# A fused two-layer perceiver kernel: router constants made in an earlier stage, a two-bank start of the causal attention, expert weights loaded in halves, and router steps moved within their slots

## The chip, the cores and the metric

The kernel runs on one core of a Trainium2 chip. The metric is the device time of one execution in microseconds (us); the time shown for a kernel is the median of its runs. Besides the timed runs there is one profiled execution, whose trace gives the start and length of every instruction on each engine: TensorE (PE, with its weight loads as PEld), VectorE (DVE), ScalarE (ACT), GpSimd (POOL) and the DMA queue that SyncE issues (SP). All arithmetic is in 32-bit floating point.

## What is computed

The input x has 64 sequences of 32 rows with 256 features (2048 tokens), and there is a context of 64 x 257 rows with 64 features. Six residual steps follow each other, each on the layer-normed x:

```python
x = x + _L0_xattn_ref(_layernorm(x), ctx_512, ...)   # 16 heads of 16, causal, first 32 context rows matter
x = x + _L0_attn_ref(_layernorm(x), ...)             # 16 heads of 128, one shared key and value
x = x + _L0_ffn_ref(_layernorm(x), ...)              # 16 blocks of 64, the top 4 kept per token
x = x + _L1_xattn_ref(_layernorm(x), ctx_512, ...)   # latent cross attention over 257 context rows, rotary keys
x = x + _L1_attn_ref(_layernorm(x), ...)             # causal, 16 heads of 16, keys and values shared by 4 heads
x = x + _L1_ffn_ref(_layernorm(x), ...)              # 8 experts, each token goes to the best one
```

The last step picks for each token the expert with the largest routing value and applies that expert's gated feed-forward block:

```python
route = jax.nn.sigmoid(x @ router_w)
max_ind = jnp.argmax(route, axis=1)
...
h = jax.nn.silu(x @ gate_w[e]) * (x @ up_w[e])
out = out + jnp.where(mask, h @ down_w[e], 0.0)
```

## The kernel before, in words

The 2048 tokens are 16 tiles x0 to x15 of 128 rows (`xf`, with four more columns for the token's number, its routing value and its norm; `xs` are the 256 features). Four tiles make a group. The stages follow each other; the program names them by letters:

- A (first causal attention), B (second attention, a loop over 16 tiles, from about 172 us), C (blocks of the first feed-forward net, from about 500 us).
- D (cross attention): a loop over 64 blocks b. `score(b)` (L1346) makes scores on PE into two banks, the negated row maximum on DVE (L1364), the exponential on ACT (L1368), its sum's reciprocal (L1376) and the product (L1377) on DVE, which leaves the probabilities `pb`. `turn(b)` transposes them on PE (L1393), `gather(b)` multiplies them with the values (L1416), `project(t)` (L1428) adds the result to x every fourth block. `steps[b]` hangs further work on a block: `ln_group(g, "d")` at block 16(g-1)+1 norms group g (so group 3 at block 33), `half` turns its rows on PE in two parts, two and six blocks later (35 and 39 for group 3); `e_values` at block 53 clears three tiles `vd` on POOL (L1243) and writes their column of ones (L1244); blocks 48 to 62 norm and turn the first rows for stage E.
- E (causal attention), from about 959 us. It has a head (`score(0)`, `values(0)`, `power(0)`, the turn and the queries of group 1) and a loop over slots t = 0 to 14. In slot t the attention of tile t+1 begins and that of tile t-1 ends: `score(t+1)` (64 small matmuls at L306, the mask and maximum on DVE at L257 and L266, the subtraction on POOL at L267), `gather(t-1)` (L1822), `values(t+1)` (L1797), `power(t+1)` (the exponential on ACT, L1789), `heads_on_partitions` of tile t (transposes at L275, copy at L277), `place_values(t+1)` (one copy on DVE at L1813, three on ACT at L1815). Between them `parts` are put in: steps of the next group's features (`transposed_part` L247, `e_features` L1261) and of the router.
- The router works on `ROUTED` sets, (0,1,2,3) and then pairs. `route_stats` takes a tile's statistics on DVE; with the set's last tile `route_scale` makes the norm's factors on POOL (L155, L156, L1594 to L1598). `route_norm` applies them on ACT (L1604), `route_turn` turns the rows on PE (L1618) with a copy on ACT (L1621), `route` makes the choice (L1630, then small DVE operations), `places` ranks the tokens (L1658, L1661), `send` scatters a tile's rows from POOL into the sorted table `srt` in DRAM (L1678). `give_out` makes the expert and row numbers of the next sorted tiles from the counts. `load_expert` (L1529) loads a third of an expert's weights, 512 KB, into `fw`; a DVE memset of one column (L1533) before it sets when SP may issue the load (L1534). Two loads stand at the end of each of slots 0 to 11.
- The expert loop follows (from about 1117 us without router work): 23 sorted tiles, each with gate, up and down matmuls, scattered into the output.

The order of instructions on an engine is the program's where a stage's `manual_schedule` lists that engine: in B it lists PE, DVE, ACT and POOL, in D PE alone, in E PE, DVE and ACT. On the others a scheduler orders them at compile time, after its own estimate of the durations. Tiles of one tag share buffers, so a new tile waits for the last reader of an old one. In stage E each of the accumulator tags "mm", "o", "v" and "PT" is one bank.

The numbers that the router and `give_out` need (`tri`, `one`, `n128`, `n128e`, `ntile`, `token`, `base`) are made between D and E: `numbers` (L1544) counts on POOL (L1546) and converts on DVE (L1548), and 16 POOL copies (L1571) put the token numbers into the tiles' column D. Memory for all these is what stage D has left.

Of the kernel before, what the change touches and what calls it, by code (L numbers as in the profile page):

```python
# [20 lines left out]
NE = 8  # L21
# [24 lines left out]
def perceiver_kernel(ctx: ExitStack, tc: tile.TileContext, a: dict, out: bass.AP):  # L46
# [119 lines left out]
    def stats(mv_slot, src, name):  # L166
        st = sm(f"lnb_{name}", [P, 6])
        nc.vector.bn_stats(st, src)
        nc.vector.bn_aggr(mv_slot, st)
# [34 lines left out]
    def ln_group(g, name, twice=False, act=False, power=False):  # L204

        mv = sm(f"lnm_{name}{g}", [P, 4, 2])
        for i in range(4):
            stats(mv[:, i, :], xs[4 * g + i], f"{name}{g}_{i}")
# [38 lines left out]
    def transposed_part(xn, xT, ps, k, name):  # L247
        tp = ps.tile([P, 512], F32, tag="mm", name=f"tp_{name}_{k}")
# [418 lines left out]


# [57 lines left out]
    with tc.tile_pool(name="wB", bufs=2) as work, tc.tile_pool(  # L726
# [174 lines left out]

        AHEAD = 10
# [69 lines left out]
        for t in range(NT + 1):  # L972
# [40 lines left out]
            place(4)  # L1013
            write_pad(t)
# [208 lines left out]
    with mbw, wd1:  # L1223
# [3 lines left out]
        with tc.tile_pool(name="wD", bufs=2) as work, tc.tile_pool(  # L1227
# [13 lines left out]
            def e_values():  # L1241
                for vd_ in vd:
                    nc.gpsimd.memset(vd_, 0.0)  # L1243
# [17 lines left out]
            def e_features(g, part, o, ps):  # L1261
# [5 lines left out]
                q_ps = ps.tile([P, 512], F32, tag="mm", name=f"qe{g}_{o}_{part}")  # L1267
# [21 lines left out]

            NB = B  # L1290
# [55 lines left out]
            def score(b):  # L1346
# [31 lines left out]
                c0 = 4 * (b % 4)  # L1378
                nc.vector.tensor_tensor(
# [69 lines left out]
            for g in range(1, NG):  # L1449
                b0 = 16 * (g - 1)  # L1450
                steps[b0 + 1] = lambda g=g: lat.update({g: ln_group(g, "d", power=g == 3)})
# [77 lines left out]
    def load_expert(e, n_):  # L1529

        key, k_ = (("f_wg", KC), ("f_wu", KC), ("f_wd", 4))[n_]
        c0 = e * FE + n_ * 1024
        nc.vector.memset(fw[:, c0 : c0 + 1], 0.0)  # L1533
        nc.sync.dma_start(  # L1534
            fw[:, c0 : c0 + 1024].rearrange("p (k i) -> p k i", k=k_),
            a[key][e].rearrange("(k p) i -> p k i", p=P),
        )

    w1 = ctx.enter_context(tc.tile_pool(name="wF1", bufs=1))


    I32 = mybir.dt.int32

    def numbers(name, pattern, mult, n):  # L1544
        i_ = w1.tile([P, n], I32, name=f"{name}_i")
        nc.gpsimd.iota(i_, pattern=pattern, base=0, channel_multiplier=mult)  # L1546
        f_ = w1.tile([P, n], F32, name=name)
        nc.vector.tensor_copy(f_, i_)  # L1548
        return f_

    tri = numbers("tri", [[1, P]], -1, P)
    nc.vector.tensor_scalar(tri, tri, 0.0, None, ALU.is_gt)
    one = w1.tile([P, P], F32, name="one")
    nc.vector.memset(one, 1.0)
    n128 = numbers("n128", [[P, NT]], 0, NT)
# [192 lines left out]
    with tc.tile_pool(name="wE", bufs=2) as work, tc.tile_pool(  # L1748
# [165 lines left out]
        for t in range(NT - 1):  # L1914
# [23 lines left out]
            for fn in parts[3:]:  # L1938
                fn()
# [257 lines left out]
```

## Time and profile before

| What | us |
|---|---|
| median of 3 runs | 1247.11 (1245.01 to 1247.27) |
| profiled execution: time | 1249.61 |
| profiled execution: span from first to last instruction | 1247.6 |
| PE busy in the span | 1178.9 (94%) |
| DVE, ACT, POOL busy | 777.5, 557.9, 367.9 |
| mean granted TensorE clock | 0.953 of full |

The profile's rows are read so. In a timeline a row is a merged run of instructions: start, length, engine, line, operation, output and inputs by the program's names with the buffer numbers left out, shape, count, and in brackets how long the engine was idle before and what released it. "issue" stands where the engine waited for nothing that the profile shows. In a table by stretches the columns are the stretch, its length, the busy time and instruction count of PE, PEld, DVE, ACT and POOL, the granted clock (1.00 is full speed), the busy share of the 16 DMA engines and the rate in GB/s. A wait for several semaphores is put down to the one that came last.

### The profile page before, as it was taken

The numbers are of one execution on the slowest core, as the hardware profiler recorded it, in microseconds if no ns is written. First come the engines' busy times: TensorE is split into PE (matmuls) and PEld (weight loads), VectorE is DVE, ScalarE is ACT, GpSimd is POOL, SyncE is SP. The second block draws the span as 40 slices with busy tenths as digits, with TensorE's granted clock in tenths as the row PEclk, the third lists the DMA queues.
The fourth block names the chain that finished last, engine by engine and source line by source line (L and its number), as shares of the span: only waits on it lengthen the run. The fifth ranks groups of instructions, "written<-read, shape, count | busy, mean of one in ns | idle before, by whom it ended". The sixth has DMA issues, their size and how long they took to land. (4 is left out here: it accounts for less than half of the span.)

```text
span 1247.6 us, 26254 instructions
## 1 busy us (share of the span) xinstructions
PE 1178.9 (94%) x10187; PEld 827.1 (66%) x10187; DVE 777.5 (62%) x1885; ACT 557.9 (45%) x1305; POOL 367.9 (29%) x472
## 2 busy tenths in 40 slices
PE   8999999999999999999989999999999698689997
PEld 5656777677767566777767777767766466555664
DVE  5766257678879966534277777676775465654332
ACT  2337354464554641222365656566654455331111
POOL 2343246675757653000010000010010356432111
PEclk8889999999999989989989999999999888789999
DMA  5121124553454454912141111111100345212110
GB/s 144 48 71 36 29 77 120 148 161 109 133 176 127 135 150 128 269 42 70 34 103 36 50 47 37 48 37 48 38 1 2 103 138 163 66 39 63 38 32 10
DMA packets 94973, 103.11 MB, mean 83 GB/s; under 512 B 37792, under 2 KB 71329, under 8 KB 94626
## 3 DMA queue, kind: packets, MB, share of 16 engines
q1 hardware_dynamic: 92978, 97.19, 27.3%
q0 software_dynamic: 1872, 4.23, 1.0%
q8 instruction: 82, 1.34, 0.4%
q14 instruction: 41, 0.34, 0.1%
HBM read 69.45 MB, written 32.85 MB: 82 GB/s over the span
## 5 line engine op out<-in xcount | busy, mean ns | idle before, releaser
L1368 ACT ACTIVATE pp<-Sd,nm 128x257 f32<-128x257 f32 x256 | 118.0, 474 | 66.5 <-DVE nm L1364 61.3
L775 PE MATMUL qb<-xT_b,b_q 128*128 128x256 f32 x512 | 122.0, 387 | 0.0
L775 PEld LDWEIGHTS qb<-xT_b,b_q 128*128 128x128 f32 x512 | 95.4, 191 | 39.3 <-issue 20.2
L866 PE MATMUL yb<-b_o,oTb 128*128 128x256 f32 x512 | 116.4, 386 | 0.0
L866 PEld LDWEIGHTS yb<-b_o,oTb 128*128 128x128 f32 x512 | 98.4, 194 | 14.3 <-issue 0.7
L1364 DVE TENSOR_REDUCE nm<-Sd 128x2 f32<-128x514 f32 x128 | 83.0, 685 | 23.2 <-PE Sd L1356 23.2
L1377 DVE TENSOR_TENSOR pp<-pp,rd 128x514 f32<-128x514 f32 x128 | 88.8, 694 | 2.1
L1399 ACT COPY pTd<-pt 128x512 f32<-128x512 f32 x112 | 61.4, 598 | 49.6 <-PE pt L1393 49.6
L794 POOL TENSOR_TENSOR q2b<-qTb 128x512 f32<-128x512 f32 x64 | 64.7, 1040 | 27.0 <-ACT qTb L783 15.7
L1416 PE MATMUL od<-pTd,na 128*64 128x256 f32 x480 | 65.2, 392 | 5.6 <-issue 4.3
L1356 PE MATMUL Sd<-ct,qTd 64*128 64x257 f32 x480 | 68.3, 403 | 0.0
L783 ACT COPY qTb<-qb 128x512 f32<-128x512 f32 x64 | 37.4, 585 | 67.8 <-PE qb L775 65.0
L1393 PE MATMUL pt<-cst,pp 128*128 128x128 f32 x512 | 67.3, 275 | 0.0
L1393 PEld LDWEIGHTS pt<-cst,pp 128*128 128x128 f32 x512 | 59.3, 142 | 9.9 <-issue 5.6
L1154 PE MATMUL qd<-xT_d,d_m 128*128 128x256 f32 x256 | 65.3, 399 | 0.2 <-ACT xT_d L242 0.2
L828 DVE RECIPROCAL rqb<-rqb 128x512 f32<-128x512 f32 x16 | 53.5, 3343 | 17.8 <-ACT rqb L823 17.8
L657 PE MATMUL yc<-c,hc 128*128 128x256 f32 x256 | 59.0, 386 | 2.6 <-DVE hc L652 2.6
L1432 PE MATMUL yd<-d_n,co 128*128 128x256 f32 x256 | 59.5, 386 | 0.0
L1154 PEld LDWEIGHTS qd<-xT_d,d_m 128*128 128x128 f32 x256 | 47.3, 194 | 17.2 <-issue 6.0
L842 DVE RECIPROCAL rdb<-denb 128x512 f32<-128x512 f32 x16 | 53.7, 3353 | 5.8 <-PE denb L840 5.6
L657 PEld LDWEIGHTS yc<-c,hc 128*128 128x128 f32 x256 | 49.1, 194 | 12.1 <-DVE hc L652 3.4
L1432 PEld LDWEIGHTS yd<-d_n,co 128*128 128x128 f32 x256 | 47.3, 190 | 11.6 <-issue 5.8
(389 smaller groups left out, 2337.7 us busy)
## 6 DMA issues: line engine op xcount, KB each, us to landing
srt<-pad SPq DMA_DIRECT2D x17, 1040.0 KB
mb<-maskd SPq DMA_DIRECT2D x64, 128.0 KB
ct<-ctd SPq DMA_DIRECT2D x30, 257.0 KB
rct<-in_ctxT_dram SPq DMA_DIRECT2D x32, 128.5 KB
rrt<-in_ctxT_dram SPq DMA_DIRECT2D x64, 64.2 KB
ctd<-rct SPq DMA_DIRECT2D x32, 128.5 KB
nad<-rna SPq DMA_DIRECT2D x16, 256.0 KB
fw<-in_f_wg_dram SPq DMA_DIRECT2D x8, 512.0 KB
```

The lines of the kernel that those rows point to most:

```text
L657: nc.tensor.matmul(y_ps, hs[f][:, i * P : (i + 1) * P], c_2[:, f, :], start=(f == 0), stop=(f == 7),)
L775: nc.tensor.matmul(q_ps[:, hh, :], b_q[:, k, h * P : (h + 1) * P], xT[:, k, c0 : c0 + 256], start=(k == 0), stop=(k == KC - 1),)
L794: nc.gpsimd.tensor_tensor(q2[:, 4 * h4 : 4 * h4 + 4, :], q, q, ALU.mult)
L866: nc.tensor.matmul(y_ps, oT[:, h, :], b_o[:, h, :], start=(h == 0), stop=(h == NH - 1))
L1154: nc.tensor.matmul(q_ps[:, r, :], m[:, k, pr * P : (pr + 1) * P], xT[:, k, c0 : c0 + 256], start=(k == 0), stop=(k == KC - 1),)
L1356: nc.tensor.matmul(s_ps[:, hh, :NKV], qT[hs, b % 8, 4 * u : 4 * u + 4, :], ct[hs, b % 4, :], start=True, stop=True,)
L1364: nc.vector.tensor_reduce(nm, s_ps[:, :, :NKV], AX.X, ALU.max, negate=True)
L1368: nc.scalar.activation(pp[:, hh, :], s_ps[:, hh, :NKV], AF.Exp, bias=nm[:, hh : hh + 1], accum_out=sd[:, hh : hh + 1],)
L1377: nc.vector.tensor_tensor(pp, pp, bc(rd, 2, NKV), ALU.mult)
L1393: nc.tensor.transpose(pt[:, hh * 256 + u * P : hh * 256 + u * P + P], probs[b][:, u, hh, c * P : (c + 1) * P], ident,)
L1416: nc.tensor.matmul(o_ps[64 * hh : 64 * hh + 64, 0, :], na[:, j, c, :], pT[:, c, hh * 256 : (hh + 1) * 256], start=(c == 0), stop=(c == 1),)
L1432: nc.tensor.matmul(y_ps, co[:, pr, :], n[:, pr, :], start=(pr == 0), stop=False)
```

## The change

It has six parts.

1. Constants. `count_up` makes the five counted tiles on POOL at the start of stage B, `all_numbers` converts them on DVE at the end of slot 2 of B into tiles that live to the end; the second count for `n128e` falls away. The 16 copies of token numbers go one by one to the ends of B's slots 3 to 16 (two in slots 3 and 16).
2. Head of E. The first turn and the queries of group 1 take two banks ("mm" and "o") in place of one; the turn stands ahead of `power(0)`, and `score(1)` stands between the turn and the queries instead of at the start of slot 0.
3. Stage D. `stats` of group 3 gets a `sign`: DVE first copies a value of the latest block's probabilities into the statistics' tile, so that the norm can't be scheduled before that block. `e_values` gets such a copy on POOL ahead of each memset. At block 33 the latest block is 34, at block 53 it is 54.
4. Weights. `load_piece` loads half of what `load_expert` did (256 KB), with its own memset; four pieces stand spread over a slot instead of two loads at its end.
5. Router in E. `route_norm` moves to the begin of its slot, right behind the scores (in slot 8 it stays behind the second part). `route_turn` does both halves at once, behind the slot's other parts: for a pair of tiles in one bank with one copy, for the first set of four in two banks.
6. Scatters. The sends move to slots 9 to 13, one behind the scores and one behind `gather`; tiles 10 and 11 are sent after the loop.

```diff
-    def stats(mv_slot, src, name):
+    def stats(mv_slot, src, name, sign=None):
         st = sm(f"lnb_{name}", [P, 6])
+        if sign is not None:
+            nc.vector.tensor_copy(st[:, 0:1], sign)
         nc.vector.bn_stats(st, src)
...
+    def count_up(pool):
+        counted = {}
+        for name, (pattern, mult, n) in COUNTS.items():
+            i_ = counted[name] = pool.tile([P, n], I32, name=f"{name}_i", bufs=1)
+            nc.gpsimd.iota(i_, pattern=pattern, base=0, channel_multiplier=mult)
+        return counted
+
+    def all_numbers(counted):
+        made = {}
+        for name, i_ in counted.items():
+            made[name] = const.tile(list(i_.shape), F32, name=name)
+            nc.vector.tensor_copy(made[name], i_)
+        tri = made["tri"]
+        nc.vector.tensor_scalar(tri, tri, 0.0, None, ALU.is_gt)
+        one = const.tile([P, P], F32, name="one")
+        nc.vector.memset(one, 1.0)
+        n128e = const.tile([P, NT], F32, name="n128e")
+        nc.vector.tensor_scalar_add(n128e, made["n128"], float(P - 1))
+        return tri, one, made["n128"], n128e, made["ntile"], made["token"], made["base"]
...
+            if t == 2:
+                tri, one, n128, n128e, ntile, token, base = all_numbers(counted)
+            if t > 2:
+                for t_ in {3: (0, 1), NT: (NT - 2, NT - 1)}.get(t, (t - 2,)):
+                    nc.gpsimd.tensor_copy(xf[t_][:, D : D + 1], token[:, t_ : t_ + 1])
             write_pad(t)
...
             def e_values():
                 for vd_ in vd:
+                    nc.gpsimd.tensor_copy(vd_[:, 0, 0, 0, 0:1], lately["p"])
                     nc.gpsimd.memset(vd_, 0.0)
...
+                lately["p"] = pb[:, 1, 1, 0:1]
...
-                steps[b0 + 1] = lambda g=g: lat.update({g: ln_group(g, "d", power=g == 3)})
+                steps[b0 + 1] = lambda g=g: lat.update(
+                    {g: ln_group(g, "d", power=g == 3, sign=lately["p"] if g == 3 else None)}
+                )
...
+    pieces = iter([(e, n_, h) for e in range(NE) for n_ in range(3) for h in range(2)])
+
+    def load_piece():
+
+        e, n_, h = next(pieces, (None,) * 3)
+        if e is None:
+            return
+        key, k_ = (("f_wg", 1), ("f_wu", 1), ("f_wd", 2))[n_]
+        c0 = e * FE + n_ * 1024 + h * 512
         nc.vector.memset(fw[:, c0 : c0 + 1], 0.0)
         nc.sync.dma_start(
-            fw[:, c0 : c0 + 1024].rearrange("p (k i) -> p k i", k=k_),
-            a[key][e].rearrange("(k p) i -> p k i", p=P),
+            fw[:, c0 : c0 + 512].rearrange("p (k i) -> p k i", k=k_),
+            a[key][e].rearrange("(k p) i -> p k i", p=P)[:, h * k_ : (h + 1) * k_, :],
         )
...
+    def route_turn(ts, work, ps, tags):
+
         n_ = len(ts)
+        xn = rows[ts]
+        xT = work.tile([P, KC, n_ * P], F32, tag="xTf", name=f"xTf{ts[0]}", bufs=1)
+        rows[ts] = xn, xT
+        ks = 4 // n_
+        for k0 in range(0, KC, ks):
+            tp = ps.tile([P, ks, n_ * P], F32, tag=tags[k0], name=f"tpf{ts[0]}_{k0}")
...
+            nc.scalar.copy(xT[:, k0 : k0 + ks, :], tp)
...
-        sends = {
-            8: (0, 1), 9: (2, 3), 10: (4, 5), 11: (6, 7), 12: (8, 9), 14: (10, 11)
-        }
+        sends = {9: (0, 1), 10: (2, 3), 11: (4, 5), 12: (6, 7), 13: (8, 9)}
...
+        e_group_start(1)
+        for k in range(KC):
+            transposed_part(lat[1], feats[1][2], ps1, k, "e1", ("mm", "o")[k])
+        score(1)
         power(0)
-        for fn in group(1, 0) + group(1, 1):
-            fn()
         place_values(0, v_ps.pop(0))
+        for o in range(KC):
+            e_features(1, 1, o, ps1, ("mm", "o")[o])
         for t in range(NT - 1):
...
-            score(t + 1)
+            if t > 0:
+                score(t + 1)
+            load_piece()
+            if t in steps_n and t % 4 > 0:
+                route_norm(steps_n[t])
+            for t_ in sends.get(t, ())[:1]:
+                send(t_)
             for fn in parts[:1]:
                 fn()
             if t > 0:
                 gather(t - 1)
-            if n_own < 2 and t in steps_n:
-                route_norm(steps_n[t])
+            load_piece()
+            for t_ in sends.get(t, ())[1:]:
+                send(t_)
             for fn in parts[1:2]:
                 fn()
-            if n_own > 1 and t in steps_n:
+            if t in steps_n and t % 4 == 0:
+
                 route_norm(steps_n[t])
...
             for fn in parts[3:]:
                 fn()
+            if t in steps_n:
+                route_turn(steps_n[t], work, ps2, ("mm", "o"))
             place_values(t + 1, v_ps.pop(t + 1))
-            for n_ in range(2 * t, 2 * t + 2):
-                if n_ < 3 * NE:
-                    load_expert(n_ // 3, n_ % 3)
+            load_piece()
...
                 route_stats(t - 1)
-            for t_ in sends.get(t, ()):
-                send(t_)
+            load_piece()
...
         gather(NT - 2)
+        for t_ in ROUTED[-3]:
+            send(t_)
         rows_turn(0)
```

## The prediction

> **What bounds the kernel now.** I read the page's 40 slices first, then busy time by stage, then the waits of the last attention stage, then the timeline at each long wait. All times are us from the span's start.
>
> The slices (engine, busy tenths; PEclk is the granted TensorE clock):
>
> ```profile
> PE   8999999999999999999989999999999698689997
> PEclk8889999999999989989989999999999888789999
> ```
>
> TensorE is busy nearly everywhere, except in slices 31 to 36, where its clock drops as well. Busy time by stage (stretch, length, busy time and count of each engine, clock, DMA share, GB/s):
>
> ```profile
> 627.00:959.00 332.00, 323.11 (x2194) 232.65 (x2194) 240.10 (x594) 203.74 (x666) 12.63 (x19) 0.99 0.17 41
> 959.00:981.40 22.40, 16.31 (x236) 9.24 (x234) 4.80 (x19) 4.19 (x8) 3.75 (x23) 0.77 0.01 2
> 981.40:1087.80 106.40, 85.19 (x2502) 62.77 (x2503) 65.85 (x233) 52.85 (x113) 56.46 (x99) 0.84 0.42 138
> 1117.00:1247.60 130.60, 123.15 (x476) 77.08 (x474) 52.74 (x135) 22.13 (x43) 24.86 (x27) 0.99 0.12 37
> ```
>
> Cross attention (627 to 959) and the expert loop (from 1117) are TensorE at full clock: nothing is won there by moving other engines' work. The causal attention loses time twice, to waits and to the clock: 22.4 us of head (score(0) to values(1)), 106.4 us of loop over slots t. The head (start, length, instruction, idle before and its releaser):
>
> ```profile
> 965.32 1.95 POOL L1571 COPY x<-token 128x1 f32<-128x1 f32 x16 [0.31 <-DVE token L1548]
> 968.31 0.63 ACT L1789 ACTIVATE s_e<-s_e 128x512 f32<-128x512 f32 x1 [9.90 <-POOL s_e L267]
> 969.46 0.72 PEld L250 LDWEIGHTS tp_e<-cst,xn_e 128*128 128x128 f32 x4 [3.48 <-ACT xT_e L251]
> 971.25 3.78 PE L1269 MATMUL qe<-xT_e,e_q 128*128 128x512 f32 x4 [0.68 <-ACT xT_e L251]
> 981.40 0.94 PEld L1797 LDWEIGHTS ve<-e_v,xT_e 128*32 128x32 f32 x64 [1.32 <-ACT vde L1815]
> ```
>
> One bank and one queue make a chain: token copies, POOL's subtract, the exponential, and only then ACT's copy that frees the bank for the second turn. The waiting TensorE goes to half clock, so four query matmuls take 3.78 instead of 1.98 us (the same group at 1006.68). In the loop:
>
> ```profile
> 994.75 0.28 PE L306 MATMUL S_e<-kde,qTe 32*32 32x64 f32 x7 [2.35 <-issue]
> 999.52 0.37 PE L1797 MATMUL ve<-e_v,xT_e 128*32 128x64 f32 x2 [2.54 <-issue]
> 1050.71 0.57 PE L1618 MATMUL tpf<-cst,xn_f 128*128 128x128 f32 x2 [1.67 <-ACT xTf L1621]
> 1074.40 1.09 ACT L1604 ACTIVATE xn_f<-x,lnq_f 128x256 f32<-128x256 f32 x2 [4.08 <-POOL lnq_f L1596]
> 1075.06 0.97 PE L1618 MATMUL tpf<-cst,xn_f 128*128 128x128 f32 x2 [4.63 <-ACT xn_f L1604]
> ```
>
> The first two waits are for nothing the program does; the third is one bank turned twice; the last waits for POOL, whose norm chain (1069.78 to 1074.4) has two scatters of 1.06 and 1.04 us inside it. Stage starts matter too; cross attention begins so:
>
> ```profile
> 624.90 1.95 POOL L1243 MEMSET vde<- 128x1088 f32 x2 [118.98 <-PE yc L657]
> 629.58 0.16 DVE L183 SCALAR_TENSOR_TENSOR lnh_d<-lnm_d,lnr_d 128x4 f32<-128x4 f32 x1 [2.40 <-POOL lnr_d L156]
> 631.46 0.50 PEld L1356 LDWEIGHTS Sd<-ct_d,qTd 64*128 64x128 f32 x4 [3.54 <-ACT pp L1368]
> ```
>
> VectorE stands at the group 3 norm, which stands behind POOL's memsets of vd; the first row maximum (L1364, 629.66) stands behind it.
>
> **Start of cross attention.** The memsets and the norm both leave this place: each now reads block probabilities of late blocks. The maximum can follow its scores at about 627.85, so the chain gains 1.8 (629.66 - 627.85); what is late next is ACT's table load, until 628.43, which allows that. The clock was half from 631.0 to 637.9; two groups there took 2.14 and 3.78 instead of 1.14 and 1.99, 2.8 in all. Whether it stays up is open (0 to -2.8); I take half: -1.4.
>
> **The norm put at block 34.** It brings to VectorE 4 copies (0.1), 4 statistics (0.43 + 0.18, overlapping, 0.5 a pair) = 2.4, then POOL's 0.23 + 1.04, then four rows at 0.47. Probabilities of block 34 are ready at 802.6 and the turn of group 3 (half(0)) needs the rows at 811.99. 802.7 + 2.4 + 1.0 (x add and statistics already there) + 1.4 + 0.2 + 1.9 = 809.6; the row maxima of the next block, at 806.91 now, stand behind it: 2.7 late, of which 1.9 (pp done 810.63, used 812.49) is slack. +1.0, between 0 (the scheduler interleaves) and +3. The vd memsets at block 54 are 3 x (1.03 + 0.3) on a POOL that is 4% busy; only VectorE can feel them: +0.3 (0 to 1). The added waits: VectorE's copy waits for VectorE itself, so for nothing; POOL's copy waits for block 54, and behind it stand only bias adds (917) and the memsets, which nobody needs before 966.
>
> **Constants moved to the second stage.** Five iotas (0.15 to 0.24 each), 8 VectorE operations of 0.17 to 0.25 (1.5) at slot 2, and 16 POOL copies of 0.12. There (212 to 232) TensorE is busy 20.00 of 20 us and POOL idles 6.1 of 20; behind the 1.5 on VectorE stand gather(2)'s copies at 230.19, whose user (L866) starts at 235.0. Covered: 0; uncovered it is +1.5 once.
>
> **Head.** Without casts the mask add starts when the scores end, 964.8 for 965.35. With two banks and the copies ahead of the exponential on ACT, in order: turns 965.6 to 966.9, xT copies to 967.6, score(1) to 967.8 (its bank is free from 965.5), queries 2 x 1.98 at full clock to 971.8, values(1) at 971.8 for 981.40. Placing value 0 on ACT (968.3 to 970.9, after VectorE's copy) is over by then. -9.6; as slot 1's oe must wait for ACT a little, -9.5 (-7.5 if the clock drops, -10).
>
> **Loop.** Weight pieces: bytes per slot are the same, 48 issues of about 0.4 on SP and 48 memsets of 0.06 on VectorE instead of 24; SP has nothing else until the rows at 1083. The two issue waits are instruction blocks: 16 of 16 KB are loaded in 979.4 to 1062.9 (the DMA answer), one per 256 instructions, while 1 MB of weights is queued. The Trainium skill, "Runtime: NRT & Kernel Launch", section "Instruction fetch mechanics", calls a block crossing "mostly hidden": by it pieces are worth 0; by the rows 4.9 us can go. The third block, with less ahead of it, started 1.1 us after its turn, the two before 2.2 and 2.3 after. I take 2 x 1.2 = -2.5, as a dense 256 instructions take about 2.3 us and no fetch is that short.
> Turns: route_turn for two tiles is one bank and one 512 copy, at the slot's end; waits of 1.15 (1034.32) and 1.67 (1050.71) go. -2.3, the longer copy (0.60 for 2 x 0.37) hidden behind the next scores.
> Norms ahead and scatters later: the 4.63 goes, as POOL runs the chain (1.9) unsplit and ACT has the whole slot. POOL per slot is then 1.06 + 0.74 + 2 x 1.2 + 1 = 5.2, under a slot's 5.5 to 8. ACT, in order, may wait at slots 11 and 13 for that chain; behind it stands only the exponential, needed a slot later.
> The clock comes on top:
>
> ```profile
> 1047.50:1050.90 3.40, 1.57 (x12) 1.25 (x12) 2.24 (x11) 2.46 (x6) 2.61 (x4) 1.00 0.84 274
> 1050.90:1061.10 10.20, 9.65 (x214) 8.03 (x214) 4.36 (x14) 4.58 (x11) 5.78 (x13) 0.50 0.43 135
> ```
>
> The Trainium skill, "TensorE: Matmul & The Clock Gate", section "HAM oscillation", gives as rule no idle gap over about 3.4 us. Here a gap of 1.67 in a window busy 1.57 of 3.40 is followed by 10.2 us at half clock. By the rule slot 10's gap is worth 1.67; by the rows another 9.65/2 at most. I take the rows, but 3.0 of it, since others pace slot 11 too. Slot 13 took 11.8 (1067.39 to 1079.19), 10.3 of it at clock 0.50, with work like slot 12's 6.5: -5.5.
> Loop: -2.5 - 2.3 - 3.0 - 5.5 = -13.3 (-6 to -20). Late next: VectorE's give(10) chain (16 operations, 1079.3 to 1082.6), then instruction blocks. After 1087.8: 0 (-2 to 1); VectorE's give(12) still holds the bank there.
>
> **Sum.** -1.8 - 1.4 + 1.0 + 0.3 - 9.5 - 13.3 = -24.7. The profiled execution took 1249.6 (span 1247.6), 2.5 over the median of 1247.1: 1249.6 - 24.7 - 2.5 = 1222.
>
> **Rivals.**
> Gaps only (0.20): the clock windows fall badly and fetches stay. -1.8 + 1.3 - 7.5 - 1.15 - 1.67 - 4.6 = -15: 1232. For it: the clock's 3.4 us windows have no fixed phase.
> Clock up throughout (0.18): -4.1 - 10 - 19 - 2 = -35: 1212. Against it: matmuls of 8 columns (L1630) precede a cold window at 1023.6 though TensorE was busy.
> Little done (0.05): POOL is not ordered by hand here; scatters land in the chain again, and the head's gain goes to later waits: 1246.
> Slower (0.11): instruction starvation. The loop's 5005 TensorE instructions are 19.6 blocks. Pieces keep weight traffic always ahead of a fetch, where now some fetches meet an empty queue. The loaded period was 4.77 (994.75 to 999.52); from 6.0 on, 118 us, the gains of head and start are eaten; at 6.3 it is 123.5: 1253. Against it: slots 11 to 14 carry almost no weights.
> Likeliest, as summed: 0.46, own range 1214 to 1230.
>
> **Numbers.** Range 1208 to 1240: it takes in the first three but for edges (0.03), and leaves out 0.05 + 0.11. About 0.2% is what a measurement of this kernel tells from no change. Faster 0.84, within 0.2% 0.05, slower 0.11.
>
> **What would show it.** Right: values(1) follows the queries without a half-clock group, about 9 us earlier; L1618's waits under 1 us; issue waits after the fourth slot under 1.5 each; L1364 starts under 1 us after the first scores. Wrong: issue waits in several slots; POOL's scatters between L155 and L1596; half(0) waiting for xn_d by over 3 us.

## The result and the profile after

The changed kernel takes 1231.11 us (median of 6 runs, 1225.71 to 1232.89), the kernel before 1246.86 in the same comparison (1239.95 to 1249.26): ratio 0.9874, 95% interval 0.9842 to 0.9906. So it is faster by 1.3%, inside the range of the prediction (1208 to 1240), 9 us above the predicted 1222 and 1 above the narrower range (1214 to 1230) of its likeliest case. The profiled execution took 1230.48, its span is 1228.4.

The 40 slices of the changed kernel's page:

```profile
PE   8999999999999989999999999989999988799997
PEclk8889999999999998988999999999999988889999
```

The weak stretch at the end of the row is shorter than before and its clock is 8 where 7 stood. By stage, in the columns of the table shown for before (cross attention, head up to the start of values(1), loop over slots, expert loop):

```profile
629.00:961.00 332.00, 321.19 (x2194) 230.42 (x2194) 240.05 (x604) 203.92 (x666) 16.01 (x24) 1.00 0.17 41
961.00:973.20 12.20, 11.96 (x238) 8.06 (x234) 4.33 (x12) 3.36 (x7) 2.10 (x2) 1.00 0.05 9
973.20:1068.80 95.60, 81.23 (x2506) 61.68 (x2506) 66.18 (x256) 53.41 (x111) 55.49 (x99) 0.89 0.51 153
1096.70:1228.40 131.70, 123.22 (x476) 77.03 (x474) 52.76 (x134) 22.14 (x43) 24.66 (x27) 0.99 0.12 37
```

Head and loop of the causal attention now take 12.2 and 95.6 us where they took 22.4 and 106.4. The head's instructions, in the timeline:

```profile
967.79 1.09 PE L252 MATMUL tp_e<-cst,xn_e 128*128 128x128 f32 x8
969.60 3.70 PE L1309 MATMUL qe<-xT_e,e_q 128*128 128x512 f32 x8
973.23 0.94 PEld L1825 LDWEIGHTS ve<-e_v,xT_e 128*32 128x32 f32 x64 [0.76 <-ACT vde L1843]
```

Eight transposes run together, the eight query matmuls take 3.70 at full clock (four took 3.78 before), and values(1) follows after 0.76. At the start of cross attention the first row maxima (VectorE) now follow their scores (TensorE) by 0.85, where they came 2.48 after them:

```profile
629.10 1.14 PE L1397 MATMUL Sd<-ct_d,qTd 64*128 64x257 f32 x8 [0.68 <-ACT qTd L1200]
629.95 1.29 DVE L1405 TENSOR_REDUCE nm<-Sd 128x2 f32<-128x514 f32 x2 [1.17 <-PE Sd L1397]
```

For the experiments I cut each profile at the same instructions: **C** from the last normed tile of stage B to the clearing of `plast`; **D start** from there to the `plast` product of block 2; **D middle** from there to that of block 62 (the expectations below call this "from the fourth block to the last"); **E head** to the first copy of turned heads; **loop** to the sixteenth such copy, with the time at half clock inside it; **rest** to the end. The `plast` product is a small one on VectorE that ends each block of D. A cold window is a stretch in which the granted TensorE clock is 0.50.

| profile | C | D start | D middle | E head | loop (half clock) | rest | span | median |
|---|---|---|---|---|---|---|---|---|
| before | 131.9 | 17.1 | 305.6 | 34.4 | 106.9 (36.1) | 157.1 | 1247.6 | 1246.9 |
| changed | 133.8 | 13.1 | 309.9 | 23.6 | 95.9 (20.5) | 157.5 | 1228.4 | 1231.1 |
| E1 norm free | 137.1 | 15.3 | 305.6 | 23.6 | 96.6 (18.6) | 157.8 | 1230.8 | 1228.8 |
| E2 two loads | 137.1 | 13.1 | 309.9 | 23.6 | 99.8 (27.3) | 156.5 | 1230.0 | 1231.4 |
| E3 old router | 137.1 | 13.1 | 309.9 | 23.6 | 112.9 (47.8) | 154.4 | 1245.1 | 1239.5 |
| E4 head alone | 131.9 | 17.1 | 305.6 | 23.6 | 108.6 (34.1) | 154.3 | 1233.6 | 1239.9 |
| E5 late weights | 137.1 | 13.1 | 309.9 | 23.6 | 94.4 (21.9) | 157.9 | 1230.6 | 1230.3 |
| E6 norm spread | 137.1 | 13.1 | 307.4 | 23.6 | 96.6 (21.7) | 158.0 | 1228.4 | 1226.5 |
| E7 old scatters | 133.8 | 13.1 | 309.9 | 23.6 | 97.9 (25.4) | 157.8 | 1226.0 | 1232.3 |
| E9 all spread | 137.1 | 13.1 | 307.9 | 23.6 | 97.8 (27.3) | 154.8 | 1226.9 | 1229.8 |
| E10 rows on GpSimd | 137.1 | 13.1 | 307.4 | 23.6 | 95.2 (20.5) | 156.5 | 1227.4 | 1227.3 |
| E11 no vd sign | 133.2 | 14.5 | 309.0 | 23.6 | 95.4 (17.5) | 156.4 | 1218.7 | 1229.1 |
| E12 vd sign alone | 131.9 | 15.0 | 305.6 | 32.0 | 106.6 (24.4) | 156.1 | 1241.9 | 1243.5 |
| E13 slack blocks | 134.6 | 14.5 | 305.4 | 23.6 | 95.1 (20.5) | 157.0 | 1220.1 | 1222.7 |

A median carries about 0.3% (4 us), while D middle and the new E head repeat to 0.1 in every profile with the same instructions there, if no cold window falls into them. Small steps are therefore read from stage lengths, and medians only say whether the sum agrees. Stages A and B (486.5 to 494.8) are not in the table: they differ between profiles by their cold windows.

### The profile page after: what moved, and what is told of

Same layout as the page of the kernel before. It is cut to its first block, busy times and chain, and to the rows that moved or that the text cites. A ratio compares the mean times of both kernels' runs of the same rounds, so it can differ in the third digit from the quotient of the medians.

```text
span 1228.4 us, 26334 instructions
## 1 busy us (share of the span) xinstructions
PE 1169.0 (95%) x10187; PEld 822.6 (67%) x10187; DVE 778.2 (63%) x1912; ACT 557.7 (45%) x1299; POOL 369.4 (30%) x474
## 3 DMA queue, kind: packets, MB, share of 16 engines
q8 instruction: 82, 1.34, 0.5%
## 5 line engine op out<-in xcount | busy, mean ns | idle before, releaser
L808 PEld LDWEIGHTS qb<-xT_b,b_q 128*128 128x128 f32 x512 | 95.4, 191 | 39.3 <-issue 20.2
L1474 PEld LDWEIGHTS yd<-d_n,co 128*128 128x128 f32 x256 | 47.3, 190 | 11.6 <-issue 5.8
```

Source lines behind the costliest of these rows:

```text
L808: nc.tensor.matmul(q_ps[:, hh, :], b_q[:, k, h * P : (h + 1) * P], xT[:, k, c0 : c0 + 256], start=(k == 0), stop=(k == KC - 1),)
L1474: nc.tensor.matmul(y_ps, co[:, pr, :], n[:, pr, :], start=(pr == 0), stop=False)
```

## The experiments

**E1, the norm of group 3 without its sign.** The vd signs stay.

```diff
-                    {g: ln_group(g, "d", power=g == 3, sign=lately["p"] if g == 3 else None)}
+                    {g: ln_group(g, "d", power=g == 3)}
```

> The changed kernel without the sign in group 3's norm (the copy of a probability that holds the norm until block 34); the three signs of the vd memsets stay. Theory A: the norm at block 34 costs the row maxima of two blocks 4.8 us (the stretch of D from the 800.1 to the 825.4 us of the changed kernel takes 25.3 against 20.5 before), so without the sign that stretch takes 20.5 to 21.5 again. At the start of D the norm stands on VectorE again, but POOL, freed of the memsets, answers in 1.3 us: at most +1.3 there. Net -3.5: 1227.5. Theory B: the 4.8 comes from the statistics of stage E's groups, which the scheduler has put into the same blocks, and goes nowhere without the sign: the stretch stays at 24 to 25 and the start gets later by 1: 1232.

1228.84 (ratio to before 0.9848, 0.9810 to 0.9886). D middle is 305.6, exactly that of before, so theory A holds: without the sign the 4.3 are gone. D start is 15.3, 2.2 more than in the changed kernel, and a cold window of 3.4 us falls into it. The changed kernel's own rows show how the 4.3 arise. A norm here is a tile's statistics (`lnb`, `lnm`) on VectorE, a factor (`lnr`) on GpSimd, a second factor (`lnh`) and the rows (`xn`) on VectorE. In the kernel before, these were the row maxima of block 35 and of block 36 (VectorE), and the scores and product behind the first of them (TensorE). VectorE had stood 1.47 for a factor of stage E right ahead of the first, but TensorE lost nothing by it:

```profile
806.91 1.28 DVE L1364 TENSOR_REDUCE nm<-Sd 128x2 f32<-128x514 f32 x2
810.75 1.29 DVE L1364 TENSOR_REDUCE nm<-Sd 128x2 f32<-128x514 f32 x2
```

```profile
809.91 1.14 PE L1356 MATMUL Sd<-ct,qTd 64*128 64x257 f32 x8
810.98 1.08 PE L1416 MATMUL od<-pTd,na 128*64 128x256 f32 x8
```

In the changed kernel, whose clock of events is here 2.5 us ahead, the same queue holds:

```profile
800.21 0.27 DVE L169 COPY lnb_d<-pp 128x1 f32<-128x1 f32 x3
...
804.35 0.16 DVE L185 SCALAR_TENSOR_TENSOR lnh_d<-lnm_d,lnr_d 128x4 f32<-128x4 f32 x1 [1.17 <-POOL lnr_d L156]
...
804.77 1.66 DVE L196 SCALAR_TENSOR_TENSOR xn_d<-x,lnr_d,lnh_d 128x256 f32<-128x256 f32 x4
806.34 1.29 DVE L1405 TENSOR_REDUCE nm<-Sd 128x2 f32<-128x514 f32 x2
...
811.30 0.16 DVE L185 SCALAR_TENSOR_TENSOR lnh_e<-lnm_e,lnr_e 128x4 f32<-128x4 f32 x1 [0.92 <-POOL lnr_e L156]
...
816.96 0.16 DVE L185 SCALAR_TENSOR_TENSOR lnh_e<-lnm_e,lnr_e 128x4 f32<-128x4 f32 x1 [1.24 <-POOL lnr_e L156]
```

The maxima at 806.34 stand behind all four statistics, VectorE's wait of 1.17 for GpSimd's factors, and four rows, so they come 1.9 late (806.34 + 2.5 - 806.91). ScalarE's exponentials wait for them, and TensorE's next scores wait for the exponentials to empty their two banks. That happens twice, and a wait put down to "issue" follows:

```profile
808.20 0.70 PE L1397 MATMUL Sd<-ct,qTd 64*128 64x257 f32 x4 [0.71 <-ACT pp L1409]
...
810.08 1.14 PE L1458 MATMUL od<-pTd,na 128*64 128x256 f32 x8 [0.26 <-ACT pTd L1441]
...
813.70 0.70 PE L1397 MATMUL Sd<-ct,qTd 64*128 64x257 f32 x4 [1.03 <-ACT pp L1409]
...
821.86 1.08 PE L1458 MATMUL od<-pTd,na 128*64 128x256 f32 x8 [1.00 <-issue]
```

In the kernel before, TensorE has no gap over 0.3 us from 800 to 824. Behind the held norm it reaches the product at 810.08 late by 1.6 (810.08 + 2.5 - 810.98). The other 2.7 of the 4.3 come at the second and third place, and there the queue stands behind the two `lnh_e` rows: the scheduler has also moved stage E's statistics and factors behind the held norm, where before it had spread the statistics singly, one about every 20 us. VectorE waits 0.92 and 1.24 for GpSimd's factors of stage E, and the next maxima stand behind each. The wait of 1.00 at 821.86 ends right after VectorE's last reading of that bank (L1370, at 821.48 and 0.28 long), so I put it down to the same queue. The sign brings the norm and stage E's factors there together, and E1 takes both away, so this split is read from the rows and not tested by itself.

**E2, the old weight loads.** Two loads of 512 KB at the end of a slot in place of four pieces.

```diff
-            load_piece()
...
+            for n_ in range(2 * t, 2 * t + 2):
+                if n_ < 3 * NE:
+                    load_expert(n_ // 3, n_ % 3)
```

> The changed kernel with the old weight loads: two of 512 KB at the end of a slot, one memset each. Theory A (the prediction): pieces shorten two waits for instruction blocks by 1.2 each; with the old loads the loop of slots takes 98.4 in place of 95.9 between the first and the last copy of turned heads, and 1233.6 in all. Theory B: pieces are worth nothing, as the changed kernel still has such waits of 3.10 and 2.12 in it: 95.9 within 1, and 1231 in all, with one or two issue waits of 2 to 3 at other places.

1231.38 (0.9877, 0.9836 to 0.9918), no difference in the median. In slots 1 to 7 the waits for instructions on TensorE are 1.80 and 1.23 here, 0.96, 3.10 and 2.12 in the changed kernel: pieces don't shorten them, so theory B for the waits. The loop of this one profile is 3.9 longer, with 6.8 more at half clock. Loops with the changed instructions span 95.9 to 97.8 (changed, E1, E6, E9), so 99.8 lies outside, and theory A named 98.4; whether it would come again one profile can't say, and 2.5 us of a median are under its noise.

**E3, the router's norm, turn and scatters at their old places.**

```diff
-            if t in steps_n and t % 4 > 0:
-                route_norm(steps_n[t])
...
+            if n_own < 2 and t in steps_n:
+                route_norm(steps_n[t])
...
-            if t in steps_n:
-                route_turn(steps_n[t], work, ps2, ("mm", "o"))
...
+                fns += [lambda k=k: route_turn(steps_n[t], k, work, ps2, "mm") for k in range(KC)]
```

> The changed kernel with the router's norm, turn and scatters at their old places in the slots (pieces, head, constants and stage D as changed). Theory A (the prediction): turns 2.3, slot 11's clock 3.0 and slot 13 5.5 come back, so the loop takes 106.7 in place of 95.9 and the whole 1242; the turn waits for POOL's norm by over 3 us at slot 13. Theory B: the loop is faster because it starts warm and without a debt behind the head, and the router's places are worth only the two turn waits: the loop takes 98 to 100, the whole 1234 to 1235.

1239.46 (0.9944, 0.9917 to 0.9971): 8.4 slower than the changed kernel. The loop took 112.9, 17 longer, 47.8 of it at half clock. Slot 13's wait is back (TensorE):

```profile
1074.97 0.97 PE L1642 MATMUL tpf<-cst,xn_f 128*128 128x128 f32 x2 [5.19 <-ACT xn_f L1628]
```

Theory A. The places of the router's steps are the main part of the loop's gain, about 8 by the medians; the 17 of one profile holds clock windows that need not fall so again.

**E4, the head alone on the kernel before,** with the constants in stage B.

```diff
-        power(0)
-        for fn in group(1, 0) + group(1, 1):
-            fn()
+        e_group_start(1)
+        for k in range(KC):
+            transposed_part(lat[1], feats[1][2], ps1, k, "e1", ("mm", "o")[k])
+        score(1)
+        power(0)
```

> The kernel before with only the constants moved to stage B and the head of E in two banks. Theory A: the head is worth 9.5 by itself and what follows keeps its length (the loop's 106.9, D's as before): 1237.4. Theory B: later waits of the loop (the POOL chain of slot 13, instruction blocks) take up a good part of it: the loop gets longer than 110, the whole 1242 to 1245.

1239.86 (0.9957, 0.9925 to 0.9990), 5 to 7 better than before; E head 23.6 in place of 34.4, the loop 108.6 in place of 106.9. The head is worth 10.8 in its own stage, and nothing else has to change for that. Whether 1.7 is given back in the loop one profile can't say. By order of size theory A.

**E5, no weights in slots 0 to 4.**

```diff
+        if t < 5:
+            return
         e, n_, h = next(pieces, (None,) * 3)
```

(and two pieces at each place from slot 5 on)

> The changed kernel with no weight piece in slots 0 to 4 of stage E; from slot 5 on two pieces stand where one stood, so that all 48 are asked for by slot 10. Theory A (the prediction): the waits for instruction blocks in slots 1 to 4 (1.28 and 2.55 in one profile, 0.96 and 3.10 in another of the changed kind) come from weights queued ahead of the block, and with no weights there they fall under 0.5 each. Theory B: a block that is fetched while 32-row matmuls rush by can't come in time by itself, weights or not: both waits stay, 1 to 3 us each, and the time stays within 3 of the changed kernel's 1231.

1230.27 (0.9821, 0.9770 to 0.9872). The waits fall from 0.96, 3.10 and 2.12 to one of 0.62, one of 1.34 (TensorE) and none near slot 6:

```profile
990.88 0.27 PE L1827 MATMUL ve<-e_v,xT_e 128*32 128x64 f32 x2 [1.34 <-issue]
```

For slots 1 to 4 this repeats: the waits over 0.6 us sum to 0.93 to 2.40 in the four profiles without weights there (E5, E10, E11, E13) and to 3.03 to 4.89 in the ten others. Past slot 4 it doesn't: with the same weights, now two pieces at each place, E10, E11 and E13 wait 2.70, 2.13 and 2.39 in slots 5 to 8. The loop is the shortest of all, 94.4, against 95.1 to 95.4 in those three. The DMA view of 975 to 1003 in 40 slices of 0.7 us shows instruction blocks and nothing else until the weights start:

```profile
GB/s 0 0 0 0 23 0 0 0 0 23 0 0 0 0 23 0 0 0 0 23 0 0 0 0 23 0 0 0 0 23 0 0 0 23 0 0 85 246 392 217
q8 instruction: 7, 0.11, 1.4%
```

One 16 KB block every five slices: the trace has them at 985.25, 988.62, 992.01, 995.44 and 998.79, 3.4 us apart. In the changed kernel they lie 3.8 to 5.0 apart over the same slots (978.64, 982.48, 986.63, 991.58, 996.21), with 198 GB/s on the queues. So both theories hold in part: weights delay the blocks, as A said, but a wait of 0.6 to 1.6 us stays without them. Whether 3.4 us is the time of a fetch or the pace at which TensorE uses blocks up is not shown. What such a wait costs beyond itself is seen in the changed kernel. First its two rows on TensorE, then the clock windows around the first of them:

```profile
989.82 0.37 PE L1825 MATMUL ve<-e_v,xT_e 128*32 128x64 f32 x2 [3.10 <-issue]
...
1018.87 0.30 PE L308 MATMUL S_e<-kde,qTe 32*32 32x64 f32 x5 [2.12 <-issue]
```

```profile
985.80:989.20 3.40, 0.92 (x66) 0.76 (x55) 1.63 (x6) 0.63 (x1) 1.75 (x3) 0.99 0.69 180
989.20:996.00 6.80, 6.18 (x136) 4.61 (x139) 3.82 (x13) 2.84 (x7) 3.37 (x4) 0.50 0.53 159
```

TensorE was busy 0.92 of 3.40 us, and the next 6.8 us ran at half clock. In E5, whose wait was 1.34, no window in slots 1 to 5 was cold (clock 1.00 over 979 to 1000), and none was in E10, E11 and E13, whose longest wait there was 1.55.

**E6, group 3's norm spread**: one tile's statistics at each of blocks 24 to 27, the scale at 28, one row at each of 29 to 32.

```diff
+            for i in range(4):
+                steps[24 + i] = lambda i=i: stats(mv3[:, i, :], xs[12 + i], f"d3_{i}", lately["p"])
+                steps[29 + i] = lambda i=i: out3(i)
+            steps[28] = scale3
```

> The changed kernel with group 3's norm of stage D spread over blocks: one tile's statistics at each of blocks 24 to 27, the scale at 28, a row at each of 29 to 32, all held by a sign of their block; the scheduler still puts stage E's eight statistics behind the last row in one bundle. Theory A: the 4.3 that the norm at block 34 costs is the length of the norm's own chain ahead of half(0); spread, the way from the fourth block to the last takes 305.6 to 306.5 in place of 309.9, the start keeps its 13.1 (17.2 before), and the whole is 1227. Theory B: about half of it is stage E's statistics, which stay in a bundle: 308, and 1229.

1226.48 (0.9824, 0.9794 to 0.9854). D middle 307.4, so 2.5 of the 4.3 are back and 1.8 stay, all of which arises at blocks 29 to 31. By size it is theory B; its reason is tried next.

**E9, stage E's statistics spread as well.**

```diff
+            for i in range(8):
+                steps[(36, 37, 38, 40, 41, 42, 43, 44)[i]] = lambda i=i: stats(
+                    mve[i // 4][:, i % 4, :], xs[i], f"e{i // 4}_{i % 4}", lately["p"]
+                )
```

> As the kernel with group 3's norm spread, and stage E's statistics of groups 0 and 1 also held by signs, one tile at a time at blocks 36 to 44. Theory A (the norm's own chain is the cost): the same 305.6 to 306.5 from the fourth block to the last, no more gained: 1227. Theory B (half of it is the bundle of stage E's statistics): 306 here against 308 with group 3's norm spread alone: 1227 against 1229. Either way the best kernel so far, if the rest stays.

1229.81 (0.9852, 0.9823 to 0.9880), D middle 307.9; up to block 32 the delay is 2.0, as in E6 (1.9). The bundle of stage E's statistics is not what stays: both theories miss.

**E10, the rows on GpSimd**, on top of E6, with E5's weights.

```diff
-                lat[3].append(ln_out(xs[12 + i], *lat["s3"], i, "d3"))
+                nc.gpsimd.tensor_scalar(
+                    y, xs[12 + i], rs3[:, i : i + 1], sh3[:, i : i + 1], ALU.mult, ALU.add
+                )
```

> The kernel with group 3's norm spread, its four rows (blocks 29 to 32) now on GpSimd in place of VectorE, and the weights as in the kernel that loads none in slots 0 to 4. Theory A: the 1.9 that the spread norm still costs between blocks 28 and 32 is VectorE's time for four rows of 0.47 in a chain where VectorE paces the blocks; on GpSimd, 4% busy there, they are free: from the fourth block to the last 305.6 to 306; with the loop's 94.4 the whole is 1222 to 1224. Theory B: it is the wait of the factors (lnh_d behind GpSimd's power) that holds VectorE, and stays: 307.4, and 1225. Theory C: GpSimd's rows take over 1.2 each and half(0) waits for them: over 308.

1227.31 (0.9831, 0.9799 to 0.9862), D middle 307.4: the rows weren't it either; theory B. Two rows of this kernel, VectorE's and then TensorE's:

```profile
779.41 0.16 DVE L185 SCALAR_TENSOR_TENSOR lnh_d<-lnm_d,lnr_d 128x4 f32<-128x4 f32 x1 [0.67 <-POOL lnr_d L156]
...
781.53 0.27 DVE L1370 TENSOR_TENSOR lT<-od,maskj 128x128 f32<-128x128 f32 x1
```

```profile
781.90 1.08 PE L1458 MATMUL od<-pTd,na 128*64 128x256 f32 x8 [1.65 <-issue]
```

VectorE stands for GpSimd between the two halves of block 29's product. Right behind that product it has a copy and the masking at 781.53 to do, and TensorE's wait of 1.65, put down to "issue", ends 0.1 after that masking has read the bank. There is little slack at that place: in the kernel before, VectorE idled 0.51 us up to the product of block 29 and 0.58 up to that of block 30, but 2.54 for block 27, 1.56 for 28, 2.56 for 31 and 3.59 for 35 (summed from its timeline between `plast` products).

**E13, each statistic in a block with slack,** and the factor `lnh` on GpSimd too, on top of E10; stage E's eight statistics are spread over six such blocks.

```diff
+                nc.gpsimd.tensor_tensor(sh, mv[:, :, 0], rs, ALU.mult)
+                nc.gpsimd.tensor_scalar(sh, sh, -1.0, None, ALU.mult)
...
+                steps[(21, 22, 25, 26)[i]] = lambda i=i: stats(
+                    mv3[:, i, :], xs[12 + i], f"d3_{i}", lately["p"]
+                )
```

> As the kernel with GpSimd's rows and late weights, but each statistic of group 3's norm in a block where VectorE idled over 1.5 us in the trace of before (blocks 23, 24, 27, 28), stage E's eight statistics likewise (blocks 31, 32, 35, 39, 40, 43), and the factor lnh of these norms on GpSimd, so that VectorE waits for GpSimd nowhere in these blocks. Theory A: what is left of the cost of the norm (1.8, all of it between blocks 28 and 31) is the place: VectorE has 0.5 us of slack in blocks 29 and 30 and its queue stood 0.67 for lnh_d there. With this the way from the fourth block to the last takes 305.6 to 306.0, as with no norm there at all, the start keeps 13.1, and the whole is 1223 to 1225, the fastest of all. Theory B: the statistics cost VectorE's path at any place: 307 to 308, and no faster than 1226.

1222.70 (0.9812, 0.9778 to 0.9846), D middle 305.4, as with no norm there. Theory A by its size; place and `lnh` changed together, so what each is worth stays open. VectorE in block 27 of this kernel:

```profile
757.64 0.43 DVE L170 BATCH_NORM_STATS2 lnb_d<-x 128x6 f32<-128x256 f32 x1
758.10 0.18 DVE L171 BATCH_NORM_AGGREGATE lnm_d<-lnb_d 128x2 f32<-128x6 f32 x1
759.13 0.42 DVE L1484 TENSOR_TENSOR x<-x,yd 128x256 f32<-128x256 f32 x1 [0.85 <-PE yd L1477]
760.65 1.29 DVE L1405 TENSOR_REDUCE nm<-Sd 128x2 f32<-128x514 f32 x2 [1.09 <-PE Sd L1397]
```

The maxima still wait for their scores, 1.09: the statistics lie in time that was idle. This is the fastest version by its median, 0.6% under the changed kernel (0.9812 / 0.9874), though the two intervals touch.

**E7, only the scatters at their old places.**

```diff
-        sends = {9: (0, 1), 10: (2, 3), 11: (4, 5), 12: (6, 7), 13: (8, 9)}
+        sends = {
+            8: (0, 1), 9: (2, 3), 10: (4, 5), 11: (6, 7), 12: (8, 9), 14: (10, 11)
+        }
```

> The changed kernel with the scatters at their old places (two at the end of slots 8 to 12 and 14), the norm and the turn of the router as changed. Theory A (the prediction): scatters inside the norm's chain on POOL make the 4.6 to 5.2 wait at slot 13; with them back there, the turn of slot 13 waits over 2, and the loop takes 100 to 103 in place of 95.9 to 96.6: 1236. Theory B: the norm at the slot's begin and the turn at its end are what removes the wait, since the chain then has the whole slot: no turn waits over 1, the loop within 1.5 of 96.3: 1231.

1232.32 (0.9889, 0.9848 to 0.9931), loop 97.9. One turn waits, that of slot 13:

```profile
1057.09 1.39 PE L1644 MATMUL tpf<-cst,xn_f 128*128 128x128 f32 x4 [2.06 <-ACT xn_f L1628]
```

Ahead of it GpSimd's chain is split again, with two scatters in it:

```profile
1052.53 1.06 POOL L1706 DMA_INDIRECT srt<-x,slots  x1 [0.50 <-POOL lnr_f L155]
1053.61 0.74 POOL L156 TENSOR_TENSOR lnr_f<-lnr_f,mhalf 128x2 f32<-128x2 f32 x1
1054.54 1.05 POOL L1706 DMA_INDIRECT srt<-x,slots  x1 [0.18 <-issue]
```

Between the two: the wait is there as A has it, but with 2.06 in place of 5.19 (E3), and the loop is 0.1 to 3.5 longer than those with all the changed places (94.4 to 97.8). The scatters' place is worth about 2 us at slot 13, not to be told from nothing by the median, and the norm's and turn's place the rest: a turn at the slot's end leaves the split chain time to finish.

**E11, without the vd signs,** on top of E10, and **E12, the vd signs alone** on the kernel before (the same line, put in).

```diff
-                    nc.gpsimd.tensor_copy(vd_[:, 0, 0, 0, 0:1], lately["p"])
                     nc.gpsimd.memset(vd_, 0.0)
```

> As the kernel before this one in the list, without the three signs ahead of the vd memsets, so the memsets stand at the start of stage D again, 4 us of GpSimd. Theory A: with no norm there, nothing of VectorE stands behind GpSimd, the start keeps its 13.1 and the whole its time (within 1); the vd signs are worth nothing once the norm is away. Theory B: [...]the order makes the first row maxima later: 14 to 17. As to stage C, whose length follows its cold clock windows alone (131.9 in the two profiles without vd signs, 133.8 to 137.1 in the eight with them): if the signs set it, 131.9 here; if it is chance, any of the three.

1229.06 (0.9852, 0.9823 to 0.9880). The first maxima start 1.16 after VectorE's queue is free for them, with the scores, as in the changed kernel (1.17); D start is 14.5 because a cold window of 3.4 us falls into it. So the vd signs are worth nothing once the norm is away. D middle is 309.0, 1.6 over E10 and all of it at the product of block 31, behind another cold window of 3.4 us.

> The kernel before with only the three signs of the vd memsets. Theory A: at the start of D the norm waits for GpSimd's factors 1.3 in place of 2.4 and more, and the start takes 15.3 as in the changed kernel without the norm's sign (17.1 before); everything else as before: -1.8, 1245. Theory B: nothing, since the clock is cold there in both: 17.1 and 1247. Stage C: 131.9 if its cold windows are chance, 133.8 to 137.1 if the signs set them.

1243.47 (0.9981, 0.9955 to 1.0007), not to be told from before by its median. D start 15.0: the factors come after 1.54 in place of 2.40, as A has it. E head is 32.0 for 34.4 because fewer cold windows fell there. Stage C is 131.9 with the signs, so they alone don't set its length.

## Why the prediction was right, step by step

The direction was right and for the main reasons given. By the profiled executions the sum was -24.7 and the measure is -19.1; the other 3 us of the 9 are the step from profile to median: I took 2.5 off, but the changed kernel's profile lies 0.6 under its own median. Of the signs that the prediction named, the queries ran at full clock, the router's turns in the loop waited 0.47 at most and the first maxima came 0.85 after their scores; but instruction waits stood in several slots, one of 2.12 after the fourth.

- **Start of cross attention**, -3.2 predicted, -4.0 measured (17.1 to 13.1). The waits gave 1.7, near the 1.8 of the prediction: counted from the clearing of `plast`, the first maxima start after 3.4 before, after 2.5 in E1 and in E12, and after 1.7 in the changed kernel, so 0.9 is GpSimd's memsets and 0.8 the norm. The other 2.3 are the clock, of which I took half of 2.8: 6.8 us at half clock fall there before, 3.4 in E1 and E12, none in the changed kernel. Some of that is luck: E11 and E13 have neither wait, but 3.4 us at half clock there, and take 14.5.
- **The norm at block 34**, +1.0 (0 to +3) predicted, +4.3 measured: this step failed, in two places. The queue itself went as worked out, even a little better: the maxima came 1.9 late and not 2.7. First, "of which 1.9 is slack" was wrong. I took it at the transposes of `pp`, the last user of the exponentials; the first users are the next block's scores, which need the two banks emptied, and the product behind them. So 1.6 of the 1.9 came through. Second, and worth more, the sum has no term for stage E's statistics and factors, which came behind the held norm: TensorE lost the other 2.7 behind them. In E6 their bundle lay elsewhere and cost nothing (E9 spread it and gained nothing), so that cost belongs to the place. E13 shows that the norm is free in the blocks where VectorE idles, with `lnh` on GpSimd.
- **The vd memsets at block 54**, +0.3 predicted, 0.0 measured: against before, the `plast` products from block 39 to 63 keep their lag within 0.1.
- **Constants**, 0 predicted, 0 measured: at the same 34.1 us of half clock in stages A and B, the last tile of B is normed at 494.4 and 494.6 with the constants at their old place (before, E12) and at 494.4 to 494.8 with the new one (E1, E5, E10).
- **Head**, -9.5 predicted, -10.8 measured (E head), alone as in company (E4). Up to 2.4 of it hangs on where cold windows fall, as the old head took 32.0 in E12. The step was the surest because it was read instruction by instruction, from released bank to next matmul.
- **Loop**, -13.3 predicted, -11.0 measured. From the start of one values(t) to the next, slot 13 gained 7.1 (5.5 predicted, though 11.8 less 6.5 is 5.3) and slot 11 2.9 (3.0 by the clock, its turn's 1.67 on top). The place of the router's steps is shown by E3, the clock's share is not. E12 has the slots of before; its loop was at half clock for 24.4 us in place of 36.1 and took 106.6 in place of 106.9. Slot 13 shows why, before and in E12, with E12's turn on TensorE below:

```profile
1063.35:1076.01 12.66, 5.66 (x181) 4.03 (x174) 7.90 (x24) 3.32 (x7) 9.24 (x17) 0.68 0.35 124
1058.11:1070.89 12.78, 5.62 (x186) 4.01 (x174) 8.12 (x25) 3.59 (x8) 9.17 (x17) 0.89 0.38 126
```

```profile
1070.08 0.97 PE L1621 MATMUL tpf<-cst,xn_f 128*128 128x128 f32 x2 [5.04 <-ACT xn_f L1607]
```

The clock is 0.68 and 0.89, the length the same: TensorE waits for the chain on GpSimd, 4.63 before and 5.04 here, and with a faster clock it only waits longer. Slot 11 took 10.7 with 6.0 us at half clock before, but 11.6 with 3.8 in E4. So the gain of slot 13 is that of the chain, and the clock alone does not tell slot 11's; what else paces that slot stays open. The instruction waits, -2.5, gained nothing: the term "2 x 1.2" was wrong. The cause behind it was right (E5: weights delay the blocks), the remedy not (E2); that half pieces put the same bytes ahead of a block, only more evenly, is the likely reason, not a tested one. The Trainium skill, "Runtime: NRT & Kernel Launch", section "Instruction fetch mechanics", holds the crossing "mostly hidden"; here it isn't: TensorE waited 0.62 and 1.34 us with no weights in flight (E5), and up to 3.37 with them (E4).
- **After the loop**, 0 predicted, +0.4 measured, within the 154.3 to 158.0 that this stretch takes over the profiles.
- **Not in the sum**: stage C got 1.9 longer at 3.4 us more of half clock, with the same instructions on TensorE in the same order. Its length follows the clock alone: with half of its time at half clock taken off it is 122.6 to 123.6 in all fourteen profiles. But it took 131.9 in all three kernels built on the one before (before, E4, E12) and 133.2 to 137.1 in all eleven built on the changed one. E4 and E12 put in the constants, the head and the vd signs and keep 131.9; E1, E2, E3 and E7 each take another part out and stay at 133.8 to 137.1. No single part sets it, and what does stays open.

The rivals: "gaps only" names 1232, next to the measured 1231, and was right that instruction waits stay. Its terms don't fit, though: -1.8 for the start (-4.0 measured), -7.5 for the head (-10.8), -7.4 for the loop (-11.0), +1.3 for the norm and the memsets (+4.3), nothing for stage C (+1.9), so that its sum is met by luck. Nor is the loop's gain one of the clock: E12's loop, at half clock for 24.4, is 10.7 longer than the changed kernel's at 20.5. "Instruction starvation" was wrong on pieces: with or without them two or three blocks are late.

## What to carry to other kernels

Ahead of moving an instruction on an in-order engine, list that engine's idle time block by block: one norm cost 4.3 us at one block together with what came behind it, 1.8 spread over neighbours, and nothing in the blocks with 1.5 us of slack and no wait for GpSimd in VectorE's queue. A wait for another engine counts against everything queued behind it; E13 put both factors and the rows on GpSimd, the engine that answers. A held instruction takes others with it: look at what the scheduler moves behind it. And where an engine waits for another's chain, don't count a faster clock on top of the wait.

## What the runs showed of the hardware

- Instruction blocks of 16 KB came 3.2 to 4.0 us apart in slots 1 to 4 with no weights in flight (E5, E10, E11, E13), and 3.5 to 5.1 with them (the ten others). The loop of the changed kernel ran 5012 TensorE instructions on 20 blocks, so a block holds about 250; the 64 matmuls and 64 weight loads of one values(t) take 1.10 us at full clock, so 250 such instructions some 2.1 us. By this estimate dense work uses up a block faster than the next one came.
- A gap of 3.10 us left TensorE busy 0.92 in a window of 3.40 and was followed by 6.8 us at half clock. In the changed kernel's loop, cut into windows of 3.4 us at the clock's own steps, those busy 0.29, 0.38, 0.49, 0.56 and 0.57 of their length were followed by half clock, those of 0.64 and more not. The longest gaps at these five were 3.10, 2.12, 2.10, 1.19 and 1.48 us: the rule of "no idle gap over about 3.4 us" that the prediction weighed (the Trainium skill, "TensorE: Matmul & The Clock Gate", section "HAM oscillation") would have called all of them safe. But no sharp line comes out of it: in E1 and in E5 a window of 0.57 was not followed by half clock.
- A busy TensorE doesn't keep its clock either. In stage C of the changed kernel it was busy 3.40 of 3.40 us from 525.0 to 528.4 (40 matmuls) and from 552.3 to 555.7 (33), and each window was followed by 10.2 us at half clock; windows of 9 and 10 longer matmuls in between ran at full clock.
- The clock's windows have no fixed phase: counted from a profile's first instruction, their grid of 3.4 us begins at 0.4 to 3.2 us over the fourteen profiles.
- A row norm (128 x 256, two scalars per row) took GpSimd 0.55 to 0.98 us, four together 2.53 to 3.02, where VectorE takes 0.47 to 0.49, and 1.66 for four.
